# Three edits where a graph-attention kernel passes from projections to gathers

## Chip, cores and metric

The kernel runs on one core of one Trainium2 chip. The time is the device time of one execution in microseconds; three runs of the kernel before gave 1809.18, 1814.11 and 1813.44 us, median 1813.44 us. The engines are TensorE (PE in the profile, its weight loads PEld), VectorE (DVE), ScalarE (ACT), GpSimd (POOL) and SyncE (SP). Each works through its own queue in order; an instruction that waits holds up all behind it. SyncE, ScalarE and GpSimd also issue transfers.

## The reference

One layer of attention over a graph of 4096 nodes with 512 features and 8 heads of 64, float32 throughout:

```python
hs, ht = layer_norm(x), layer_norm(h_target)
q = (ht @ Wq + bq) / sqrt(64); k = hs @ Wk + bk; v = hs @ Wv + bv
logits = where(adj != 0, q . k, -1e30)            # per head, 4096 x 4096
ht = ht + (softmax(logits) @ v) @ Wo + bo
ht = layer_norm(ht)
out = layernorm(x + ht + gelu(ht @ W1) @ W2)      # W1: 512 x 2048
```

adj is sparse: a row has about 17 entries, at most some 39.

## The kernel before

The kernel does not form the 4096 x 4096 logits. It has two phases.

**Phase 1.** The function `project` goes through x in 16 groups of two tiles of 128 rows. For each tile, `source` multiplies the normed, transposed rows by Wk and Wv (L929), ScalarE copies the two halves out of PSUM (L931), and ScalarE's queue writes the k|v rows, 128 x 1024, to the table `kvd` in DRAM (L935). At the same time `edges` turns adj into lists of neighbours, tile by tile of 128 rows, each in four quarters of 1024 columns: SyncE loads a quarter (`quarter`, L713), ScalarE takes its sign and counts it (L728), VectorE multiplies by positions (L733) and takes the eight largest of five segments (L735); at a tile's end VectorE merges them (L742 to L759), and the leftover goes to DRAM (L766). There are 32 tiles, so 128 quarters; I number the quarters 0 to 127. After the first 16 tiles (half A), `sort` ranks the rows by degree, and GpSimd scatters the lists as records to DRAM (L853, 16 transfers). After these, `first_fronts` starts the q rows of the first two sorted tiles.

**Phase 2.** `attention` takes the sorted tiles in 211 chunks of up to three neighbours. GpSimd gathers the k|v rows of each neighbour, 128 rows of 4 KB, from `kvd` into slots of a ring (L966); VectorE multiplies k by q (L1220) and sums by head (L1225); ScalarE takes exp and scales a third of the values (L1204); VectorE scales the others (L1184); TensorE sums the values by transposing products into PSUM (L1192). `finish` and `feed` do Wo, the second norm and the feed-forward part (L1325, L1334). The lists of half B that are not yet made are made meanwhile.

**The ring.** `ring` has 20 slots of 1024 floats for each partition. In phase 1 it is lent out: slots 0 to 7 hold adjacency quarters (`DEEP` = 8), 8 to 11 rows of h_target and later 8 to 10 the last k|v rows, 12 to 16 rows of x (`xrows`). Slots 17 and 18 are `wide`; quarters from tile NA + FILL on take these two in turn, so the load of a quarter waits until the sign of the quarter two before it has been taken. In phase 2 the gathers of half A use slots 0 to 16, and `place` says which slots each chunk gets; a chunk that doesn't fit before the end of the ring starts again at 0.

**Order.** The generators are woven together by the costs that they yield; a scheduler then sets the order in each engine's queue. Two things steer it near the change. `fill` makes `FILL` tiles of half B's lists in phase 1; `other_lists` makes the rest. And `front`, which makes the q rows of a tile, begins with a tie: VectorE's L994 reads the norm factors in the record and, formally, the tile named in `latest`, so it can't come before that tile is there. ScalarE's L998 then scales the gathered row, TensorE transposes it (L1002), ScalarE copies (L1005), TensorE multiplies by Wq (L1011), VectorE adds the bias (L1016). `latest` is set in `source`, and `first_fronts` goes on as soon as it is set:

```python
tie = nc.vector.scalar_tensor_tensor(m, m, latest[-1], m, op0=ALU.bypass, op1=ALU.max)
...
while not latest:
    yield None
```

Of the kernel before, what the change touches and what calls it, by code (L numbers as in the profile page):

```python
# [423 lines left out]
def _take(gen, n):  # L424

    for _ in range(n):
        cost = next(gen, StopIteration)
        if cost is StopIteration:
            return
        yield cost  # L430
# [13 lines left out]
def adj_resnorm_kernel(  # L444
# [38 lines left out]
    NT = N // P  # L483
    G = 2
# [48 lines left out]
    with tc.tile_pool(name="keep", bufs=1) as keep:  # L533
# [17 lines left out]
        with ExitStack() as late:  # L551
# [151 lines left out]

            adjs = []
            DEEP = 8
            FILL = 5

            def quarter(i, h):
                if i < NA + FILL:
                    a = ring[:, (i * NQ + h) % DEEP, :].bitcast(I32)  # L710
                else:
                    a = turn_of("wide", wide)
                nc.sync.dma_start(a, adj[i * P:(i + 1) * P, h * QW:(h + 1) * QW])  # L713
                return a

            def edges(i):
# [4 lines left out]
                for h in range(NQ):  # L721
# [7 lines left out]
                    ahead = min(n + DEEP - 1, n + 3 + n // 2)  # L729
                    while len(adjs) < min(max(n + 3, min(ahead, (NA + FILL) * NQ)), NT * NQ):  # L730
                        adjs.append(quarter(*divmod(len(adjs), NQ)))
# [132 lines left out]
            def project(order, t=None):  # L864
# [54 lines left out]
                def source(n, j):  # L919
                    g, hT = order[n], state[n][1]  # L920
                    if asked or moms:
                        kvr = sp.tile([P, 2 * D], F32, name="tq", bufs=3)
                    else:

                        kvr = ring[:, 8 + (n * G + j) % 3, :]
                    for half, w in enumerate((wk, wv)):
                        pkv = psi.tile([P, D], F32, name="pq", bufs=3)
                        for kc in range(KC):
                            nc.tensor.matmul(pkv, hT[:, kc, j * P:(j + 1) * P], w[:, kc, :],  # L929
                                             start=kc == 0, stop=kc == KC - 1)  # L930
                        nc.scalar.copy(kvr[:, half * D:(half + 1) * D], pkv)  # L931
                    if n >= 14:
                        latest[:] = [kvr[:, 0:1]]
                    r0 = 1 + (g * G + j) * P
                    newest[:] = [nc.scalar.dma_start(kvd[r0:r0 + P, :], kvr).ins]  # L935
                    return 7.8
# [13 lines left out]
                for n in range(len(order)):  # L950
                    for j in range(G):
                        cost = source(n, j)
                        if j == 0:
                            request(n + 4)
                            measure(n + 3)
                            turn(n + 1)
                        else:
                            scale(n + 2)
                            del state[n]
                        yield cost  # L960
# [9 lines left out]
            def prefetch(i):  # L970
                if i >= NT or i in recs:
                    return
                r0 = TILES[i][0]
                part = 1 if r0 >= PARTS[1][0] * P else 0
                assert part in done
                r0 -= PARTS[part][0] * P
                rec = sp.tile([P, E0 + MAXE], I32, name="rec", bufs=6)

                nc.gpsimd.dma_start(rec[:, :RW], recs_d[part][r0:r0 + P, :])
                recs[i] = rec  # L980

            def front(i, idle=0):


                rec = recs[i]
                tq = sp.tile([P, 2 * D], F32, name="tq", bufs=3)
                t = tq[:, :D]
                gather(t, h_target, rec[:, TGT:TGT + 1])
                for _ in range(1 + idle):
                    yield  # L990


                m = rec[:, RST:RST + 2].bitcast(F32)
                tie = nc.vector.scalar_tensor_tensor(m, m, latest[-1], m, op0=ALU.bypass,  # L994
                                                     op1=ALU.max)
                with tc.issue_after(tie.ins):
                    nc.vector.tensor_copy(tags[:, i, :], rec[:, DEG:TGT + 1])
                nc.scalar.activation(t, t, AF.Identity, bias=m[:, 1:2], scale=m[:, 0:1])  # L998
                yield
                pt = ps.tile([P, KC, P], F32, name="t", bufs=2)  # L1000
                for kc in range(KC):
                    nc.tensor.transpose(pt[:, kc, :], t[:, kc * P:(kc + 1) * P], ident)  # L1002
                hT = tq[:, D:].rearrange("p (c t) -> p c t", c=KC)
                for kc in range(KC):
                    nc.scalar.activation(hT[:, kc, :], pt[:, kc, :], AF.Identity,  # L1005
                                         bias=b1r[:, kc:kc + 1], scale=s1c[:, kc:kc + 1])
                yield
                yield
                pq = ps.tile([P, D], F32, name="t", bufs=2)
                for kc in range(KC):  # L1010
                    nc.tensor.matmul(pq, hT[:, kc, :], wq[:, kc, :], start=kc == 0,  # L1011
                                     stop=kc == KC - 1)
                yield
                yield
                yield
                nc.vector.scalar_tensor_tensor(tq[:, :D], pq, HD ** -0.5, bqr,  # L1016
                                               op0=ALU.mult, op1=ALU.add)
                tqs[i] = tq

            EARLY = 2  # L1020
# [1 line left out]
            SG = [(i, j0, min(S, cap - j0)) for i, (_, cap) in enumerate(TILES)  # L1022
                  for j0 in range(0, cap, S)]
            kvs, rests, fronts = {}, {}, {}
            place = [0]
            for i, _, n in SG:
                if place[-1] + n > RING[i >= NA]:
                    place[-1] = 0
# [6 lines left out]
            def step(gens, i):  # L1035

                if i in gens and next(gens[i], StopIteration) is StopIteration:
                    del gens[i]
# [111 lines left out]
            def go_on():  # L1150
                for i in list(fronts):
                    step(fronts, i)

            def first_fronts():

                for i in range(EARLY):
                    prefetch(i)
                for i in range(EARLY):
                    fronts[i] = front(i)
                    step(fronts, i)  # L1160
                while not latest:
                    yield None
                while fronts:
                    go_on()
                    yield 4.0
# [235 lines left out]
            def prepare():  # L1401

                yield from _take(ed, NA * steps)
                ready.append("lists")
                while moms:
                    moments(moms.pop(0))
                rs, nm = rstd_of(wp, mvh, NT, "n0")
                for R, (i0, n) in zip(Rs, PARTS):
                    Rf = R.bitcast(F32)
                    nc.vector.tensor_copy(Rf[:, :, RST], rs[:, i0:i0 + n])  # L1410
                    nc.vector.tensor_copy(Rf[:, :, RST + 1], nm[:, i0:i0 + n])
                nm = turn_of("wide", wide)
                nc.sync.dma_start(nm[:NT, :P], nodemask.rearrange("(c p) -> c p", p=P))
                nmf = nm.bitcast(F32)[:NT, P:2 * P]
                nc.vector.tensor_scalar(nmf, nm[:NT, :P], 1.0, None, op0=ALU.not_equal)
                nc.vector.tensor_reduce(bad[:NT, 0:1], nmf, AX.X, ALU.max)
                yield from sort(0)
                yield from first_fronts()

            def fill():  # L1420
# [3 lines left out]
                yield 9.0  # L1424
                for cost in _take(ed, FILL * steps):
                    yield cost
# [60 lines left out]
```

## Time and profile before

| | before |
|---|---|
| median of three runs | 1813.44 us |
| the profiled execution, its span | 1811.19 us, 1809.4 us |
| TensorE busy, of the span | 1681.5 us, 93% |
| VectorE, ScalarE, GpSimd busy | 1435.1, 1221.1, 979.8 us |
| moved from and to DRAM | 463.26 MB, mean 256 GB/s |
| last k\|v row's write issued (L935) | 290.03 us |
| first gather of k\|v rows issued (L966) | 296.81 us |
| first attention multiply (L1220) | 308.02 us |

Times in the timeline are microseconds from the start of the span. A line of it gives the start, the duration, the engine, the line of the program and the operation; in brackets at the end stand how long the engine had been idle, and what ended that. Lines with a letter q (SPq, ACTq) are transfers being issued. A wait for several things is put down to the one that the profile saw end last. The table of windows gives busy microseconds for each engine in a stretch of time, with the number of instructions, the granted clock of TensorE (1.00 is full) and the share of the DMA engines that was busy.

### The profile page before, as it was taken

The page shows a single profiled execution, that of the slowest core. Times are in us where ns is not written, and L with a number is a line of the kernel's source. Part 1 is how long each engine was busy: PE and PEld are TensorE (multiplying, and loading weights), DVE is VectorE, ACT ScalarE, POOL GpSimd, SP SyncE. Part 2 cuts the span into 40 slices and gives each one's busy share as a digit, 9 for nine tenths or more (in the row PEclk, how much of TensorE's full clock was granted, in tenths as well). Part 3 has the DMA queues.
Part 4 walks back from the last instruction along what each step waited for, and adds up shares of the span by engine and source line. Part 5 has one row for each costly group of instructions (what it writes and reads, how often), then busy time and mean ns, then how long its engine had stood idle before and what let it go on. Part 6 is the DMA issues. An engine that isn't in the chain of part 4 may idle for free. (4 is left out here: it accounts for less than half of the span.)

```text
span 1809.4 us, 22969 instructions
## 1 busy us (share of the span) xinstructions
PE 1681.5 (93%) x7030; PEld 1101.4 (61%) x7030; DVE 1435.1 (79%) x2660; ACT 1221.1 (67%) x3119; POOL 979.8 (54%) x834
## 2 busy tenths in 40 slices
PE   7989984587999989999999989999999999999997
PEld 3434432465766666676776757666666666666664
DVE  6989886899999837777879989979879797988200
ACT  5767654486997636767768867877777676787211
POOL 1000144666566576667767788877575665663101
PEclk9999996698999999999999999999999999999998
DMA  9999968988887647778879888787776777774000
GB/s 343 370 376 375 344 228 293 405 276 321 294 300 237 230 159 258 240 253 279 281 256 320 288 263 292 252 281 261 242 273 216 255 239 247 247 246 149 18 6 26
DMA packets 140268, 463.26 MB, mean 256 GB/s; under 512 B 16500, under 2 KB 21672, under 8 KB 140136
## 3 DMA queue, kind: packets, MB, share of 16 engines
q0 software_dynamic: 96656, 342.64, 55.9%
q1 hardware_dynamic: 35664, 95.98, 15.0%
q10 hardware_dynamic: 7816, 23.08, 3.3%
q8 instruction: 58, 0.95, 0.2%
q14 instruction: 74, 0.61, 0.1%
HBM read 430.75 MB, written 30.89 MB: 255 GB/s over the span
## 5 line engine op out<-in xcount | busy, mean ns | idle before, releaser
L966 POOL DMA_INDIRECT kv<-kvd,rec x603 | 761.1, 1262 | 366.9 <-PE cps L1192 147.8
L1334 PE MATMUL po<-w,gt 128*128 128x512 f32 x1024 | 466.9, 598 | 10.3 <-ACT gt L1328 10.3
L1325 PE MATMUL pf<-h2T,w 128*128 128x256 f32 (+1 forms) x2176 | 466.5, 368 | 0.0
L1325 PEld LDWEIGHTS pf<-h2T,w 128*128 128x128 f32 x2176 | 389.7, 191 | 64.4 <-issue 19.8
L1220 DVE TENSOR_TENSOR kv<-kv,tq 128x1536 f32<-128x1536 f32 (+2 forms) x211 | 352.0, 1677 | 62.0 <-DMA kv<-kvd,rec 57.9
L1204 ACT ACTIVATE kv<-kv,pa 128x64 f32<-128x64 f32 x1520 | 390.9, 337 | 4.5
L1225 DVE TENSOR_REDUCE lg<-kv 128x24 f32<-128x1536 f32 (+2 forms) x211 | 350.4, 1668 | 1.2
L1334 PEld LDWEIGHTS po<-w,gt 128*128 128x128 f32 x1024 | 189.1, 192 | 207.2 <-issue 195.3
L1192 PE MATMUL cps<-ident,kv 128*128 128x128 f32 x2008 | 267.8, 282 | 47.7 <-DVE kv L1184 40.0
L1192 PEld LDWEIGHTS cps<-ident,kv 128*128 128x128 f32 x2008 | 242.2, 146 | 114.0 <-DVE kv L1184 45.8
L1184 DVE TENSOR_TENSOR kv<-kv,p 128x1024 f32<-128x1024 f32 (+1 forms) x211 | 251.3, 1195 | 23.8 <-ACT p L1229 22.5
L687 POOL TENSOR_TENSOR n_rs<-n_ve,mhalf 128x2 f32<-128x2 f32 (+2 forms) x51 | 48.6, 953 | 326.0 <-DVE n_ve L680 173.0
L728 ACT ACTIVATE kv<-kv 128x1024 uint8<-128x1024 int32 x128 | 134.9, 1055 | 94.5 <-DMA kv<-in_adj_dram 42.9
L1328 ACT ACTIVATE gt<-pf 128x512 f32<-128x512 f32 x128 | 76.3, 597 | 87.4 <-PE pf L1325 84.0
L1328 ACT ACT_TABLE_LOAD x103 | 132.1, 1283 | 1.7
L735 DVE MAX8 cand<-kv 128x8 uint16<-128x103 uint16 (+1 forms) x640 | 132.4, 253 | 0.5
L929 PE MATMUL pq<-wk,h2T 128*128 128x512 f32 x256 | 121.3, 619 | 8.3 <-ACT tq L931 5.7
L1229 ACT ACTIVATE p<-lg 128x24 f32<-128x24 f32 (+2 forms) x179 | 39.1, 218 | 120.5 <-DVE lg L1225 119.7
L1011 PE MATMUL t<-wq,tq 128*128 128x512 f32 x256 | 115.7, 595 | 2.1 <-ACT tq L1005 2.1
L929 PE MATMUL pq<-wv,h2T 128*128 128x512 f32 x256 | 115.4, 593 | 1.8 <-DVE rbc L662 1.0
L1115 PE MATMUL t<-wo,rb 128*128 128x512 f32 x256 | 115.2, 592 | 0.0
L929 PEld LDWEIGHTS pq<-wk,h2T 128*128 128x128 f32 x256 | 49.4, 199 | 65.3 <-issue 50.5
(160 smaller groups left out, 1581.8 us busy)
## 6 DMA issues: line engine op xcount, KB each, us to landing
kv<-in_adj_dram SPq DMA_DIRECT2D x128, 512.0 KB, 7.1
kvd<-tq ACTq DMA_DIRECT2D x24, 512.0 KB, 6.6
kv<-kvd,rec POOLq DMA_INDIRECT x603, 5.9
kv<-in_L_gnn_h_target_dram SPq DMA_DIRECT2D x32, 256.0 KB, 8.0
kv<-in_x_dram SPq DMA_DIRECT2D x15, 512.0 KB, 9.3
rest_d<-gid SPq DMA_DIRECT2D x32, 160.0 KB, 4.7
w<-in_L_gnn_W_dram SPq DMA_DIRECT2D x4, 1024.0 KB, 9.9
kvd<-kv ACTq DMA_DIRECT2D x8, 512.0 KB, 5.2
```

The lines of the kernel that those rows point to most:

```text
L728: nc.scalar.activation(sg, a, AF.Sign, accum_out=dpart[:, i, h:h + 1])
L735: nc.vector.max(cand[:, h * SQ + s, :], wd[:, w0:w1])
L929: nc.tensor.matmul(pkv, hT[:, kc, j * P:(j + 1) * P], w[:, kc, :], start=kc == 0, stop=kc == KC - 1)
L966: nc.gpsimd.indirect_dma_start(out=dst, out_offset=None, in_=table[:, :], in_offset=bass.IndirectOffsetOnAxis(ap=idx, axis=0))
L1184: nc.vector.tensor_tensor(v4, v4, p[:, j0:j0 + m, :].unsqueeze(3) .to_broadcast([P, m, H, HD]), ALU.mult)
L1192: nc.tensor.matmul(cps[:, c, :], kv[:, j, D + c * P:D + (c + 1) * P], ident, is_transpose=True, start=j0 + j == 0 and c == 0, stop=j0 + n ...
L1204: newest[:] = [nc.scalar.mul(v, v, pa[:, hd:hd + 1]).ins]
L1220: nc.vector.tensor_tensor(kv[:, :n, :D], kv[:, :n, :D], tq[:, :D].unsqueeze(1).to_broadcast([P, n, D]), ALU.mult)
L1225: nc.vector.tensor_reduce(lg[:, :n, :], kv[:, :n, :D].rearrange("p j (h d) -> p j h d", h=H), AX.X, ALU.add)
L1325: nc.tensor.matmul(pf[:, k, :], w1[(f0 + k) // KC][:, kc, (f0 + k) % KC * P:((f0 + k) % KC + 1) * P], h2T[:, kc, :w], start=kc == 0, stop= ...
L1328: nc.scalar.activation(gt, pf, AF.Gelu_apprx_tanh)
L1334: nc.tensor.matmul(po[j], gt[:, k, j * P:(j + 1) * P], w2[(f0 + k) // KC][:, (f0 + k) % KC, :], start=False, stop=f0 + k == FC - 1, skip_g ...
```

## The change

There are four edits. `FILL` goes from 5 to 4, so tile 20 of the lists is left to `other_lists` and its quarters use the two wide slots. `latest` is set only by the very last k|v row, where it was set by each row of the last two groups. The first chunk's gathers start at ring slot 11 in place of 0, so the first two chunks take slots 11 to 16, and all later places shift. And the loops that fetch the first two records and start the first two fronts are merged.

```diff
             DEEP = 8
-            FILL = 5
+            FILL = 4
...
-                    if n >= 14:
+                    if n * G + j == NT - 1:
                         latest[:] = [kvr[:, 0:1]]
...
-            place = [0]
+            place = [11]
             for i, _, n in SG:
                 if place[-1] + n > RING[i >= NA]:
                     place[-1] = 0
...
                 for i in range(EARLY):
                     prefetch(i)
-                for i in range(EARLY):
                     fronts[i] = front(i)
                     step(fronts, i)
                 while not latest:
```

## The prediction, before the result was known

> **What bounds the kernel now.** I read the windows first: busy time of each engine by stretch, with the granted clock and the DMA share.
>
> ```profile
> core 0: us, PE busy (x) PEld busy (x) DVE busy (x) ACT busy (x) POOL busy (x), PEclk, DMA share, GB/s
> 297.00:350.00 53.00, 15.90 (x64) 12.87 (x65) 40.08 (x68) 20.99 (x71) 35.61 (x30) 0.50 1.02 392
> 400.00:450.00 50.00, 40.83 (x205) 29.43 (x204) 48.95 (x112) 33.95 (x96) 32.67 (x27) 0.86 0.88 314
> 450.00:500.00 50.00, 50.00 (x227) 35.20 (x226) 46.13 (x109) 45.63 (x110) 27.64 (x23) 1.00 0.85 288
> 1500.00:1600.00 100.00, 100.00 (x434) 68.32 (x434) 81.25 (x94) 72.59 (x192) 62.66 (x53) 1.00 0.76 256
> ```
>
> Three regimes follow one another. From the first gather (297) to 350 the transfers are the bound: DMA share 1.02, TensorE busy 15.9 of 53 us at half clock. To about 450 VectorE is (48.95 of 50), fed by attention and by the lists still to be made. After that TensorE is full to the end: 1403 of the 1459 us from 350 on are busy. So a microsecond by which the first gather moves should reach the end nearly whole. What sets the first gather is in the timeline, ahead of it:
>
> ```profile
> 262.61 1.06 ACT L728 ACTIVATE kv<-kv 128x1024 uint8<-128x1024 int32 x1 [2.23 <-DMA kv<-in_adj_dram]
> 268.84 0.22 DVE L994 SCALAR_TENSOR_TENSOR rec<-rec,kv 128x2 f32<-128x2 f32 x1 [6.78 <-DMA rec<-rec]
> 273.06 0.81 ACT L998 ACTIVATE tq<-tq,rec 128x512 f32<-128x512 f32 x1 [9.30 <-DVE gid L750]
> 273.93 1.11 PE L1002 MATMUL t<-ident,tq 128*128 128x128 f32 x4 [7.91 <-ACT tq L998]
> ...
> 286.82 0.62 ACT L931 COPY kv<-pq 128x512 f32<-128x512 f32 x1
> ...
> 290.03 0.33 ACTq L935 DMA_DIRECT2D kvd<-kv  x1
> ...
> 296.81 0.96 POOL L966 DMA_INDIRECT kv<-kvd,rec  x1 [20.42 <-ACT kv L728]
> ...
> 308.02 1.77 DVE L1220 TENSOR_TENSOR kv<-kv,tq 128x1536 f32<-128x1536 f32 x1 [1.98 <-DMA kv<-kvd,rec]
> ```
>
> The tie (L994) stands in VectorE's queue long before its record has landed: VectorE stops 6.78 us, ScalarE 9.30, TensorE 7.91, and the last two k|v rows stand behind them. The last row is copied from 286.82, its write to kvd issued at 290.03, landed 6.0 us later by the answer for that line, and 0.8 us after that POOL issues the first gather. The page names ScalarE's L728 as releaser; but the adjacency quarters that held slots 0 to 2 were read by 248.7, so I take the landing, which all gathers need.
>
> **What the skill says.** The Trainium skill, "DMA: Bandwidth & Descriptors", section "Issuing engines are not separate DMA queues": transfers of ScalarE, SyncE and GpSimd run on the same 16 engines and interleave. The trace agrees: share 1.02 while all three issue. "Anatomy of one DMA — SWDGE (gpsimd) path" gives about 2.0 us plus bytes/436e3. For a 512 KB quarter that is, as an estimate, 3.2 us, below the 3.8 to 6.3 us measured here; I use the measured ones. "TensorE: Matmul & The Clock Gate", section "What's actually happening": half clock after an idle window of some 3.4 us. The trace agrees (PEclk 0.50 from 297 to 350), and it costs nothing there, since DMA is the bound.
>
> **The change, part by part**, against the profiled execution's 1811.19 us (span 1809.4; the median shown is 1813.44, 2.25 above it; gains are taken from the median).
>
> *The tie.* The compiled order puts L994 and L998 behind the copy of the last row's k half (L931), and TensorE's L1002 behind both products of that row. L994 now waits for a record that landed at 268.8 at the latest, so the 6.78, 9.30 and 7.91 us go. Behind the tie stand the maxima of later lists, which nobody needs there; behind L998 stands the row's v half, which then waits for the quarter ahead of it, below.
>
> *FILL 5 to 4.* Quarters 80 to 83 (tile 20) leave the eight slots and take the two wide ones, which before began at 84. A wide quarter costs a round trip: sign 1.06, 0.12 until SyncE issues the load of the next but one (254.54 to 254.66), landing, 0.1. Four landings of quiet time can be read: 3.8 (issued 242.3), 6.3 (256.2), 5.5 (276.85 to the sign at 282.38), 4.6 (279.4): mean 5.0, so 6.3 us for each two quarters. ScalarE's queue after the change holds quarters 80 to 92 among the last copies; SyncE's loads follow in their order. From 80 at 245.6 and 81 at 246.7: 82 at 251.9, 83 at 253.6 (behind a copy), 84 at 258.2; then two copies and four L914 (3.2 us), 85 at 262.7; 86 at 264.5, 87 at 269.0, 88 at 270.8, 89 at 275.3, 90 at 277.1. The last row's k half is copied at 278.2; 91 at 281.6, two L998 to 284.2, 92 at 284.2, v half copied at 285.3, its write issued at 286.0. Before: 290.03. Gain 4.0; the first gather at about 292.8. TensorE follows: three pq buffers let the last row's products run at 269 to 276, before the copies want them. The eight L1005 and L1011 end at about 294, ahead of the first gathered rows (292.8 plus 11.2, as 296.81 to 308.02 before).
>
> *Work handed on.* VectorE's order has 97 quarters ahead of the sixth gathered chunk in both versions; after it, the changed kernel is 3 quarters behind at the 24th chunk (105 against 108) and level at the 30th (116). A quarter costs VectorE 0.41 + 0.93 us and a quarter of a tile's 4.1 us end: 2.4. So VectorE has up to 7.2 us less to do where it is the bound (TensorE waits some 9 us between 428 and 442) and 7.2 more from 460 to 520, where it had about 4 us free. The bounds are 7 gained and 3 lost; I take 1 gained, since most returns soon.
>
> *place = [11].* Six first chunks still have 17 slots of their own; slots 11 to 16 were last read by transposes or as h rows that are long done. The adjacency waits of the first gathers go, but they were not the last to end: 0. If they had been, 1 to 2 us. Counting over all 211 chunks, a slot's last user lies five chunks back for 54 of A's chunks (56 before), and never nearer: 0.
>
> *The merged loop.* The compiled POOL queue still has five record loads and then the three row gathers: 0. The x gathers for the end (2 x 1 us on POOL) now wait for the later tags, at about 280, and stand ahead of the first gather; they end by 283, before 292.8. A landing that came 10 us sooner would uncover them.
>
> Sum: 4.0 + 1 = 5 us, 1806.2 for the profiled execution, **1808.4 against the median**.
>
> **Rivals.** *The two slots take the tie's place*: each microsecond of landing is paid about five times in the chain 80, 82, ... 92. At 5.8 us the gain is nil: 1813.4. For it: 6.3 is in the trace, when a row's write was in flight; against: 3.8 and 4.6 as well. *Slower*: the same chain, place ScalarE's queue from 246 to 290, at the 7.1 us measured with the DMA full (222 to 226): 11 us later instead of 4 earlier, so 7 lost, 1820. It decides from a mean landing of 6.8 us on (5.4 lost). Against it: these 13 quarters and some rows are about 10 MB in 45 us, some 220 GB/s, where the windows from 45 to 180 moved 370. *VectorE's relief stays*: the early chunks gain most of the 7.2 us and the later ones pay it from slack: 4 + 7, so 1802. For it: TensorE's 9 us of waits; against: VectorE at 46 to 49 of 50 us right after. *The change does nothing*, because L728 is the true releaser: then removing it gains too, so that isn't apart from the first case.
>
> **How the numbers follow.** Likeliest 0.50, 1808.4, with its own range 1804 to 1812; no gain 0.20; slower 0.15; relief 0.15. About 0.3%, 5.4 us, is what a measurement of this kernel can tell from no change: faster lies below 1808.0. Faster: 0.50 x 0.5 + 0.15 = 0.40. Slower, above 1818.9: 0.15, and 0.03 of the others for an order on TensorE that I can't cost. Same 0.42. The range reaches from the relief to the slow chain: 1799 to 1820.
>
> **What would show it.** Right: no 7 us gap at L994, L998 or L1002; the last kvd write at about 286; the first gather at about 293 with the landing or nothing behind it; L728 waiting for adjacency loads about ten times for 3 to 5 us between 246 and 290; the first L1220 at 304; from there the same windows some 4 us sooner. Wrong: ScalarE's waits of 5 us and more for quarters 82 to 92, or an L998 that waits for its tie to be freed; or TensorE idle for more than 16 us between 400 and 500, from list work that now falls there.

## The result, and the profile after

| | before | after |
|---|---|---|
| median | 1813.78 us (4 runs, 1809.18 to 1814.74) | 1831.51 us (4 runs, 1826.58 to 1834.99) |
| the profiled execution, its span | 1811.19 us, 1809.4 us | 1834.99 us, 1833.2 us |
| last k\|v row's write issued (L935) | 290.03 us | 287.02 us |
| first gather of k\|v rows issued (L966) | 296.81 us | 293.90 us |
| first attention multiply | 308.02 us | 304.48 us |

The changed kernel is slower: after over before is 1.0101, 95% interval 1.0071 to 1.0131. Forecast were 1808.4 us, with a range from 1799 to 1820. From line 1158 on the changed program's numbers are one lower: L1220 of before is L1219 of after, L1225 is L1224, L1334 is L1333.

The start came out within 1.1 us of the forecast at all three of these times. These are lines of the timeline of after:

```profile
251.03 1.06 ACT L728 ACTIVATE kv<-kv 128x1024 uint8<-128x1024 int32 x1 [3.89 <-DMA kv<-in_adj_dram]
...
258.13 1.06 ACT L728 ACTIVATE kv<-kv 128x1024 uint8<-128x1024 int32 x1 [3.77 <-DMA kv<-in_adj_dram]
...
283.28 1.50 ACT L998 ACTIVATE tq<-tq,rec 128x512 f32<-128x512 f32 x2
...
284.13 1.97 PE L1002 MATMUL t<-ident,tq 128*128 128x128 f32 x8 [8.08 <-ACT tq L998]
...
287.02 0.33 ACTq L935 DMA_DIRECT2D kvd<-kv  x1
...
293.90 0.94 POOL L966 DMA_INDIRECT kv<-kvd,rec  x1 [11.50 <-DMA rest_d<-gid]
...
304.48 1.76 DVE L1219 TENSOR_TENSOR kv<-kv,tq 128x1536 f32<-128x1536 f32 x1 [7.03 <-DMA kv<-kvd,rec]
```

The stalls of 6.78 and 9.30 us at L994 and L998 are gone; ScalarE waits instead for the loads through two slots, 3.9 and 3.8 us here, and all the same issues the last row 3.0 us sooner. TensorE still waits ahead of L1002, 8.08 us (7.91 in before), but the products of all k|v rows now stand ahead of that wait. So the loss lies later. The windows of after show where:

```profile
core 0: us, PE busy (x) PEld busy (x) DVE busy (x) ACT busy (x) POOL busy (x), PEclk, DMA share, GB/s
400.00:450.00 50.00, 37.86 (x188) 27.87 (x187) 46.28 (x96) 35.34 (x105) 34.25 (x28) 0.83 0.90 322
450.00:500.00 50.00, 48.88 (x221) 34.48 (x220) 43.12 (x102) 41.37 (x98) 26.18 (x21) 1.00 0.76 257
500.00:550.00 50.00, 44.64 (x187) 29.46 (x188) 46.40 (x115) 40.34 (x99) 24.02 (x20) 0.93 0.72 245
600.00:700.00 100.00, 92.11 (x420) 63.74 (x419) 75.42 (x91) 59.33 (x166) 56.36 (x49) 0.97 0.61 201
```

and of before, for the two stretches that the prediction did not show:

```profile
500.00:550.00 50.00, 48.15 (x213) 32.39 (x212) 49.43 (x123) 43.18 (x105) 29.53 (x24) 1.00 0.88 306
600.00:700.00 100.00, 92.97 (x414) 63.20 (x413) 62.34 (x72) 59.16 (x164) 67.01 (x61) 0.97 0.59 199
```

From 400 to 450 VectorE was relieved (46.28 us busy instead of 48.95), and TensorE did less, not more (37.86 instead of 40.83). From 500 to 550 TensorE is busy 3.5 us less. From 600 to 650 it is 4.8 us less (43.89 against 48.69), but from 600 to 700 only 0.9. What it waits for after 600 is in the timeline of after:

```profile
598.11 0.92 DVE L735 MAX8 cand<-kv 128x8 uint16<-128x103 uint16 x5
...
604.46 0.96 DVE L827 TENSOR_TENSOR kv<-kv,bins 128x768 bf16<-128x768 bf16 x1
605.33 0.68 DVE L1016 SCALAR_TENSOR_TENSOR tq<-t,bqr 128x512 f32<-128x512 f32 x1
...
618.28 0.81 ACT L1133 ACTIVATE h<-h,n_nm,n_rs 128x512 f32<-128x512 f32 x1 [1.16 <-DVE n_nm L692]
...
623.10 1.04 PE L1142 MATMUL t<-ident,h 128*128 128x128 f32 x8
...
630.04 1.93 ACT L1146 ACTIVATE h2T<-t,cols 128x256 f32<-128x256 f32 x4
...
631.11 1.12 PE L1098 MATMUL t<-ident,rb 128*128 128x128 f32 x4 [6.11 <-ACT h2T L1146]
632.02 5.28 PE L1333 MATMUL po<-w,gt 128*128 128x512 f32 x6
```

and the same chain in before:

```profile
586.88 0.95 DVE L827 TENSOR_TENSOR kv<-kv,bins 128x768 bf16<-128x768 bf16 x1
...
591.67 0.69 DVE L1016 SCALAR_TENSOR_TENSOR tq<-t,bqr 128x512 f32<-128x512 f32 x1 [3.09 <-PE t L1011]
...
604.63 0.81 ACT L1133 ACTIVATE h<-h,n_nm,n_rs 128x512 f32<-128x512 f32 x1 [0.83 <-DVE n_nm L692]
...
614.25 1.04 PE L1142 MATMUL t<-ident,h 128*128 128x128 f32 x8
...
616.39 1.93 ACT L1146 ACTIVATE h2T<-t,cols 128x256 f32<-128x256 f32 x4
...
617.46 0.66 PE L1098 MATMUL t<-ident,rb 128*128 128x128 f32 x4 [1.31 <-ACT h2T L1146]
```

After is 13.7 us late at L1016 and 13.65 at ScalarE's h of the second norm (L1133) and at its h2T (L1146), the transposed rows for the feed-forward part. TensorE's transposes of h (L1142) are only 8.85 us late and done at 624.1; h2T comes at 630.04, because it stands in ScalarE's queue behind the exps and scales of two chunks, and ScalarE has no gap between L1133 and L1146. In before, VectorE had the lists behind it by then, and at L1016 it waited 3.09 us for TensorE. In after, the last quarter's maxima (L735, at 598), its tile's end and the first step of the second sort (to L827) stand in VectorE's queue ahead of L1016, and nothing is left of that margin. TensorE was 8.85 us late at L1142; the other 4.8 are the wait of 6.11 in place of 1.31.

This wait is no net loss, though. Before has one like it 36 us later, for ScalarE's gelu (gt), which after has not; hence the 0.9 us from 600 to 700:

```profile
667.49 5.29 PE L1334 MATMUL po<-w,gt 128*128 128x512 f32 x6 [5.43 <-ACT gt L1328]
```

What stays lost lies one group earlier, where the same links show in after,

```profile
503.98 1.76 DVE L735 MAX8 cand<-kv 128x8 uint16<-128x103 uint16 x10
...
508.54 0.68 DVE L1016 SCALAR_TENSOR_TENSOR tq<-t,bqr 128x512 f32<-128x512 f32 x1
...
525.10 0.16 DVE L692 SCALAR_TENSOR_TENSOR n_nm<-mv,n_rs 128x2 f32<-128x2 f32 x1 [0.62 <-POOL n_rs L687]
...
533.25 1.11 PE L1098 MATMUL t<-ident,rb 128*128 128x128 f32 x4 [4.54 <-ACT h2T L1146]
```

and in before:

```profile
502.44 0.68 DVE L1016 SCALAR_TENSOR_TENSOR tq<-t,bqr 128x512 f32<-128x512 f32 x1
...
514.00 0.16 DVE L692 SCALAR_TENSOR_TENSOR n_nm<-mv,n_rs 128x2 f32<-128x2 f32 x1 [0.57 <-POOL n_rs L687]
...
527.53 0.66 PE L1098 MATMUL t<-ident,rb 128*128 128x128 f32 x4 [1.85 <-ACT h2T L1146]
```

The maxima of two quarters stand in one row at 503.98, L1016 is 6.1 us late, the norm's last step on VectorE (L692) 11.1, and TensorE's wait is 4.54 us in place of 1.85.

VectorE's compiled order shows how the lists came there. In before, one quarter (its L733) stands between the 30th and 31st chunk, three between the 36th and 37th, none between the 42nd and 43rd. In after these are five, seven and three. The 30th, 36th and 42nd chunk end a tile. The multiplies of the traces say the same: after is 1.1 us ahead at the 30th (494.46 against 495.55), 10.55 us behind at the 37th (560.06 against 549.51), 13.65 at the 43rd (606.05 against 592.40).

### The profile page after: what moved, and what is told of

Same layout as the page of the kernel before. It is cut to its first block, busy times and chain, and to the rows that moved or that the text cites. A ratio compares the mean times of both kernels' runs of the same rounds, so it can differ in the third digit from the quotient of the medians.

```text
span 1833.2 us, 22964 instructions
## 1 busy us (share of the span) xinstructions
PE 1691.0 (92%) x7030; PEld 1103.2 (60%) x7030; DVE 1437.3 (78%) x2660; ACT 1217.3 (66%) x3115; POOL 985.4 (54%) x834
## 5 line engine op out<-in xcount | busy, mean ns | idle before, releaser
L966 POOL DMA_INDIRECT kv<-kvd,rec x603 | 763.0, 1265 | 354.9 <-PE cps L1191 142.9
L1333 PE MATMUL po<-w,gt 128*128 128x512 f32 x1024 | 469.5, 601 | 7.3 <-ACT gt L1327 7.3
L1219 DVE TENSOR_TENSOR kv<-kv,tq 128x1536 f32<-128x1536 f32 (+2 forms) x211 | 351.9, 1677 | 83.3 <-DMA kv<-kvd,rec 71.6
L1224 DVE TENSOR_REDUCE lg<-kv 128x24 f32<-128x1536 f32 (+2 forms) x211 | 350.1, 1668 | 1.3
L1333 PEld LDWEIGHTS po<-w,gt 128*128 128x128 f32 x1024 | 190.2, 193 | 205.8 <-issue 196.6
L687 POOL TENSOR_TENSOR n_rs<-n_ve,mhalf 128x2 f32<-128x2 f32 (+2 forms) x51 | 52.5, 1029 | 338.3 <-DVE n_ve L680 183.0
L735 DVE MAX8 cand<-kv 128x8 uint16<-128x103 uint16 (+1 forms) x640 | 132.1, 253 | 0.7
L1011 PE MATMUL t<-wq,tq 128*128 128x512 f32 x256 | 119.4, 610 | 8.7 <-ACT tq L1005 8.7
```

Source lines behind the costliest of these rows:

```text
L735: nc.vector.max(cand[:, h * SQ + s, :], wd[:, w0:w1])
L966: nc.gpsimd.indirect_dma_start(out=dst, out_offset=None, in_=table[:, :], in_offset=bass.IndirectOffsetOnAxis(ap=idx, axis=0))
L1219: nc.vector.tensor_tensor(kv[:, :n, :D], kv[:, :n, :D], tq[:, :D].unsqueeze(1).to_broadcast([P, n, D]), ALU.mult)
L1224: nc.vector.tensor_reduce(lg[:, :n, :], kv[:, :n, :D].rearrange("p j (h d) -> p j h d", h=H), AX.X, ALU.add)
L1333: nc.tensor.matmul(po[j], gt[:, k, j * P:(j + 1) * P], w2[(f0 + k) // KC][:, (f0 + k) % KC, :], start=False, stop=f0 + k == FC - 1, skip_g ...
```

## The experiments

Single executions of one kernel lie 5 us and more from their median, and two traces of the changed kernel have spans of 1833.2 and 1824.4 us. So differences are taken between medians or ratios, and traces only for the place of a loss. Ratios are to the kernel before on the same chip. "The tie" below is the change to `latest`.

**The edits one by one, and FILL undone.** Theory A: the lists handed on by FILL cost. B: the gather slots (place). C: no edit carries it, only compiled orders.

```diff
-            FILL = 5
+            FILL = 4
```


> The kernel before with FILL 4 alone (tie and place as before). Theory A, list work: the quarters that the two slots make three later return after the first group of tiles, when TensorE is already the bound, so this edit alone carries the loss: 1826 to 1836 us, with TensorE's busy time per 50 us down by 3 to 5 us somewhere between 430 and 700. Theory B, ring: the offset of the gather slots carries it, so this is 1811 to 1817. Theory C, order: no edit carries it alone, the compiled orders of VectorE and ScalarE differ with each, and this is anywhere in 1808 to 1826.

```diff
-                    if n >= 14:
+                    if n * G + j == NT - 1:
```


> The kernel before with the tie moved to the last k|v row alone. Every theory: the 7 us gaps of VectorE, ScalarE and TensorE at L994, L998 and L1002 go, and the last write to kvd is issued 3 to 8 us sooner than 290.0, since no two-slot chain stands in its way. A and B: this reaches the end, 1805 to 1811. C: it may reach the end or be lost, 1805 to 1822.

```diff
-            place = [0]
+            place = [11]
```


> The kernel before with the first gathers' slots begun at 11 alone. Theory A: 1811 to 1817, nothing. Theory B: slots whose readers are still at work hold gathers back, 1826 to 1836, with VectorE's wait for gathered rows 10 us and more above the 57.9 of the kernel before. Theory C: 1808 to 1826, with no gather that waits for its slot.

The last starts from the changed kernel:

```diff
-            FILL = 4
+            FILL = 5
```


> The changed kernel with FILL set back to 5 (tie, place and the merged loop stay). Theory A: the loss goes and the gain of the start stays, 1804 to 1811. Theory B: the loss stays, 1826 to 1836. Theory C: somewhere between, 1808 to 1830, and not the sum of the single edits.

| run | median us | ratio, 95% interval |
|---|---|---|
| FILL alone | 1825.51 | 1.0067 (1.0042 to 1.0091) |
| tie alone | 1807.29 | 0.9964 (0.9950 to 0.9978) |
| place alone | 1817.35 | 1.0024 (1.0012 to 1.0035) |
| all but FILL | 1811.72 | 0.9984 (0.9967 to 1.0002) |

FILL carries most of the loss and the tie is a gain, as A says, though FILL alone stayed 0.5 us short of its band and the run without FILL lies 0.7 above its own. The tie's write to kvd was issued at 287.28, 2.75 us sooner than before, where 3 to 8 were expected, and TensorE's wait ahead of L1002, which was expected to go, is 9.51 us. FILL alone starts late: its first multiply comes at 312.37, 4.35 us after that of before, and its TensorE is busy 8.7 us less from 600 to 650, where A had 3 to 5. Place costs about 4, which A had as nothing, and far less than B had. Without FILL, tie and place add up: -6.2 and +3.9 make -2.3, measured -1.8.

**What of FILL costs.** FILL 4 does two things: four quarters more go through the two wide slots, and the stream of later lists is one tile longer, so everything in it, the second sort too, comes 18 units later (four quarters at 3, a tile's end at 6) in the plan that weaves it with attention, where a group of two tiles counts 60. The first run has the tie and FILL together (and the merged loop); the other three start from the tie alone and separate the two.

```diff
-            place = [11]
+            place = [0]
```


> The changed kernel with place set back to 0: the tie and FILL 4 together. If the three edits' effects add (tie 6.2 gained, FILL 12.0 lost, place 3.9 lost, from the single edits) this is 1819, and the changed kernel should have been 1823. If the two slots take the tie's gain in the start, so that FILL costs more beside the tie, this is 1825 to 1829, and place is the rest.

```diff
-                if i < NA + FILL:
+                if i < NA + FILL - 1:
...
-                    while len(adjs) < min(max(n + 3, min(ahead, (NA + FILL) * NQ)), NT * NQ):
+                    while len(adjs) < min(max(n + 3, min(ahead, (NA + FILL - 1) * NQ)), NT * NQ):
```


> The kernel with the tie on the last row alone (1807.3), where tile 20's quarters also take the two wide slots, as with FILL 4, but all lists keep their planned times, as with FILL 5. Theory of the two slots: what FILL costs is the chain of loads through two slots ahead of the first gather, so this is 1816 to 1823, with the last write to kvd 4 us or more later than without. Theory of the delay: the cost is that lists, the second sort and its scatters are planned 18 units later, so this is 1804 to 1812.

```diff
-            WAIT = 40.0
+            WAIT = 58.0
```


> The kernel with the tie on the last row alone (1807.3), with FILL 5 and every slot as it was, but with the other lists' stream begun at 58 units in place of 40: the 18 units (4 quarters of 3 and a tile's end of 6) by which one tile more delays it. Theory of the delay: 1816 to 1823, with the second sort at the 51st chunk, its last scatter at 700 us or later in place of 661, and TensorE waiting for h2T or rb of a tile's end between 500 and 660. Theory of the two slots: 1804 to 1811.

```diff
-            FILL = 5
+            FILL = 4
...
-            WAIT = 40.0
+            WAIT = 22.0
```


> The kernel with the tie on the last row alone (1807.3), with FILL 4, and the other lists' stream begun at 22 units in place of 40, so that each later list and the second sort keep the places that they have with FILL 5. Theory of the delay: the loss goes, 1804 to 1812. Theory of the two slots: the loss stays, 1816 to 1823.

| run | median us | ratio, 95% interval |
|---|---|---|
| tie and FILL 4 | 1821.80 | 1.0046 (1.0029 to 1.0063) |
| tie, wide slots from tile 20 on | 1810.13 | 0.9983 (0.9970 to 0.9997) |
| tie, lists 18 units later | 1820.65 | 1.0045 (1.0029 to 1.0061) |
| tie, FILL 4, lists 18 units sooner | 1812.09 | 0.9987 (0.9971 to 1.0003) |

This decides it. With five tiles made ahead, the same slots and the same work, the delay alone costs 13.4 us; FILL 4 without the delay costs 4.8, of which the slots are 2.8 (the intervals touch that of the tie alone). The two slots are out as the main cause. The parts overlap: 4.8 and 13.4 make 18.2, where FILL 4 whole costs 14.5 beside the tie. The tie and FILL together lie between the sum of the single edits (1819) and the case that the slots take the tie's gain (from 1825), nearer to the sum. The windows of the tie alone,

```profile
420.00:450.00 30.00, 20.49 (x91) 15.52 (x89) 30.00 (x58) 19.60 (x57) 19.83 (x17) 0.77 0.94 347
500.00:550.00 50.00, 48.21 (x217) 32.67 (x216) 49.44 (x115) 42.15 (x100) 27.49 (x22) 1.00 0.86 305
```

and of the tie with the delay:

```profile
420.00:450.00 30.00, 17.48 (x96) 13.24 (x95) 25.46 (x41) 20.19 (x57) 20.74 (x16) 0.83 0.95 355
500.00:550.00 50.00, 44.16 (x187) 29.43 (x186) 43.99 (x103) 39.68 (x96) 18.72 (x18) 0.93 0.69 239
```

From 420 to 450 VectorE is freed of 4.5 us, and TensorE loses 3.0; from 500 to 550 TensorE loses 4.1, though VectorE is busy 5.5 us less. In after the same freedom was not used either: its TensorE waited 6.80 us for rb, a tile's inverse softmax sums, at 432 (2.68 in before) with the DMA share at 0.96 from 420 to 450 (0.93 in before).

How far TensorE is behind the tie alone, at the first matrix product of each tile's end (L1111), in single traces, in us, tiles counted from 0:

| tile in order | 2 | 4 | 5 | 7 | 8 | 11 | 31 |
|---|---|---|---|---|---|---|---|
| tie with the delay | 1.4 | 1.7 | 9.4 | 18.1 | 10.5 | 14.6 | 13.7 |
| the changed kernel | 0.1 | 4.1 | 10.3 | 20.8 | 13.2 | 20.1 | 22.5 |

The delay alone draws the curve of the changed kernel: up at tile 5, up at tile 7, that second rise back at tile 8, and up at tile 11. The rise at 5 is the link shown at 533; that at 7 is the wait at 631 (630.3 with the delay), and it goes back because the tie alone has its own wait later, 4.82 us for ScalarE's gelu at 664.64. The cause of the rise at 11 stays open. The last scatter of the tie with the delay came at 717.7 us, where the tie alone has 660.5.

**The changed kernel again, the sort alone late, and lists sooner.** The first run is unaltered; the others start from the tie alone.

> The changed kernel once more, unaltered, so that its time stands beside the others' with as many runs. The tie and FILL 4 together gave 1821.8. If place costs beside them what it costs alone (3.9) or beside the tie (4.4), this is 1824 to 1828; if it costs the whole distance to the first measurement, 1830 to 1834.

```diff
                 keep_rest()
+                yield 18.0
                 yield from sort(1)
```


> The kernel with the tie alone (1807.3) with 18 units of pause put ahead of the second sort: the lists keep their places, the sort goes from the 48th chunk to the 51st as with the delay of everything (1820.7). If the loss comes from the lists' own maxima, which stand in VectorE's queue ahead of a group's end, this is 1806 to 1811. If it comes from the sort, its 16 scatters and the records they write, 1815 to 1822.

```diff
-            WAIT = 40.0
+            WAIT = 22.0
```


> The kernel with the tie alone (1807.3), FILL 5, with the other lists' stream begun at 22 units in place of 40: the opposite of the delay, lists and sort some 3 to 6 chunks sooner. If a later stream simply costs and an earlier one gains, this is 1797 to 1804. If 40 is near the best, because before 450 VectorE has no room, it is 1807 to 1818, with VectorE full and TensorE idle between 400 and 450.

```diff
-            FILL = 5
+            FILL = 6
```


> The kernel with the tie alone (1807.3) with FILL 6: one tile of lists more made ahead, and all later ones 18 units sooner. Theory of the delay, as for the stream begun at 22 units: the compiled order of VectorE puts the same quarters at the same chunks, so this is within 3 us of that run; theory of the amount made ahead: it is 5 us or more better than that run.

| run | median us | ratio, 95% interval |
|---|---|---|
| the changed kernel again | 1828.98 | 1.0089 (1.0062 to 1.0116) |
| tie, sort alone later | 1805.27 | 0.9940 (0.9920 to 0.9961) |
| tie, lists 18 units sooner | 1808.81 | 0.9968 (0.9953 to 0.9983) |
| tie, FILL 6 | 1812.85 | 0.9985 (0.9964 to 1.0005) |

A later sort costs nothing (it came out 0.7 below its band): it is the lists. Their loads, signs and maxima move together in all these runs; that the maxima do it is read from the traces and shown by no run. The changed kernel itself lies between its two bands. Sooner lists gain nothing. FILL 6 missed its band of 3 us above or below the run with sooner lists by 1 (4.0 higher), with overlapping intervals; that more lists made ahead would help is out. The tie with the later sort beats both kernels; against the tie alone its intervals overlap.

**Late, or stacked? And place.** Two more starts for the stream, from the tie alone, and two more places, in the changed kernel.

```diff
-            WAIT = 40.0
+            WAIT = 64.0
```


> The kernel with the tie alone (1807.3), FILL 5, the other lists' stream begun at 64 units. It is later than at 58 (1820.7; the sort at the 52nd chunk instead of the 51st), but its compiled order spreads the lists: quarters 112 to 115 stand between the 30th and 35th chunk, and 120 to 123 between the 36th and 40th, where at 58 eight quarters stand at the 30th and eight at the 36th. Theory of lateness: 1820 to 1826. Theory of stacking: 1809 to 1816.

```diff
-            WAIT = 40.0
+            WAIT = 46.0
```


> The kernel with the tie alone (1807.3), FILL 5, the other lists' stream begun at 46 units: a third of the delay of 58, with the sort at the 48th chunk as without. Its order has four quarters at the 30th chunk and eight between the 35th and 36th. Theory of lateness: about a third of the loss, 1809 to 1814. Theory of stacking: between, 1810 to 1817, with the loss at the 36th chunk and none at the 30th.

```diff
-            place = [11]
+            place = [14]
```


> The changed kernel with place 14 instead of 11: the first chunk still goes to slots that held x, and the slots of all later chunks are shifted as well. Its compiled order has quarters 112 to 115 at the 35th chunk, as with place 0 (1821.8), where place 11 has them at the 30th (1829 to 1831). Theory that place acts through the lists' position: 1818 to 1825. Theory that it acts through the slots: 1827 to 1833.

```diff
-            place = [11]
+            place = [3]
```


> The changed kernel with place 3 instead of 11: no slot of x is used for the first chunk, but the slots are shifted against place 0. The lists stand as with place 0. Theory of the lists' position: 1818 to 1825. Theory that any shift of the slots costs: 1826 to 1833.

| run | median us | ratio, 95% interval |
|---|---|---|
| tie, stream from 64 | 1823.53 | 1.0046 (1.0029 to 1.0063) |
| tie, stream from 46 | 1818.28 | 1.0033 (1.0022 to 1.0044) |
| changed kernel, place 14 | 1829.32 | 1.0100 (1.0070 to 1.0131) |
| changed kernel, place 3 | 1828.21 | 1.0082 (1.0055 to 1.0108) |

Stacking is not decided. The run at 64 was to spread the lists, but in its trace five quarters stand between the 30th and 31st chunk and six between the 36th and 37th, as many as at 58. FILL alone speaks against it, with two and three there and 12.0 us lost, of which 4.35 ahead of its first multiply. Lateness is right in kind, not in proportion: a third of the delay (46) has most of the loss, more than either theory gave it. TensorE's one wait, summed from 480 to 660, grows with these four starts (the trace at 46 is of an execution of 1814.41 us, 3.9 below its median). The columns are the total, the number of waits, the longest; the traces are those of the stream begun at 40,

```profile
PE t L1098 <- ACT h2T L1146: 3.1, 2, 1.8
```

at 46,

```profile
PE t L1098 <- ACT h2T L1146: 5.8, 2, 4.4
```

at 58,

```profile
PE t L1098 <- ACT h2T L1146: 9.2, 2, 6.1
```

and at 64:

```profile
PE t L1098 <- ACT h2T L1146: 11.6, 2, 7.5
```

It does not measure the loss, though. With the stream begun at 22 it is 7.9, and that run is within 2 us of the one begun at 40:

```profile
PE t L1098 <- ACT h2T L1146: 7.9, 2, 6.3
```

So how the late lists come to cost TensorE 13 us is shown only in part, at 533.

For place, the lists' position is out: with 3 and 14 the lists stand nearly as with place 0, yet it is 1828 to 1829 and not 1821.8. So are the slots of x for the first gathers: place 3 gives the first three chunks none of them and costs the same. What remains is that each shift of the slots that was tried costs: the three values other than 0 cost 6 to 10 us beside the tie and FILL 4. How it does that stays open: no single place in the traces shows it.

**Undoing one thing in the changed kernel itself.**

```diff
-            WAIT = 40.0
+            WAIT = 22.0
```


> The changed kernel with all its edits, but with the other lists' stream begun at 22 units in place of 40, which gives the later lists and the second sort the places that they had before. If the delay is the main cause of its loss, this is 13 us or more below the changed kernel (1829 to 1831): 1811 to 1818. If place or the two slots carry it, 1822 to 1831.

```diff
-                    if n * G + j == NT - 1:
+                    if n >= 14:
```


> The changed kernel with the tie put back on the last two groups of rows, FILL 4 and place 11 kept. If the tie gains in it what it gains alone (6.2) or beside FILL 4 (3.7): 1832 to 1837. If its gain at the start is swallowed by the late lists: 1827 to 1832.

| run | median us | ratio, 95% interval |
|---|---|---|
| changed kernel, lists 18 units sooner | 1816.69 | 1.0039 (1.0023 to 1.0055) |
| changed kernel, old tie | 1842.46 | 1.0167 (1.0143 to 1.0191) |

With the lists back in time, 12.3 us (against the second measurement of the changed kernel) to 14.8 (against the first) return; by ratios, each to the kernel before on its own chip, 9 to 11. The wait is back to where it was:

```profile
PE t L1098 <- ACT h2T L1146: 2.5, 2, 1.3
```

The old tie costs 11 to 13.5 in the changed kernel, about twice what it costs alone (6.2): beyond its band. Its first multiply comes at 310.16, 5.7 us after that of the changed kernel. So the tie's gain is not swallowed, and the sizes depend on each other.

## Why the prediction was wrong, step by step

- **What bounds the kernel, and the first gather.** Held in kind: with the tie alone the gain of the start reaches the end. It is not one for one: the first multiply came at 305.19, 2.8 us sooner, and the median is 6.2 lower.
- **The tie.** Held but for TensorE's 7.91 us, which did not go (8.08 at L1002) and cost nothing that I can see: no stall at L994 or L998, last write 287.02 (forecast 286.0), first gather 293.90 (292.8), first multiply 304.48 (304).
- **FILL, the chain through two slots.** Held in the start: quarters 82, 85, 88 and 91 were taken at 251.03, 261.98, 270.68 and 282.23, forecast 251.9, 262.7, 270.8 and 281.6. The slower rival put the loss here; the loss came, but from here only 2.8 us, with the tie.
- **Work handed on: the step that failed.** I had bounds of 7 gained and 3 lost and took 1 gained, "since most returns soon". The delay alone measured 13.4 lost. Three things were wrong. I counted quarters per chunk up to the 30th, where after was "level" only with the five quarters that stand behind that chunk (ahead of it, as I had counted at the 24th, it is 112 against 116), and did not go on: the 36th and 42nd chunk take seven and three. I priced the work by room, "about 4 us free" against 7.2, where position counts: behind the lists in VectorE's queue stands the chain of a group's second norm, which in before has no margin at 502 and 3.09 us at 592. The traces show that at 533; for the rest of the 13.4 us the way to TensorE stays open. And I booked a relief ahead of 450 as TensorE's gain; VectorE idled instead. The case for the relief as a rival falls with it.
- **place = [11].** Taken as 0, which failed too; it is 3.9 alone and 7 to 10 in the changed kernel, from a cause that stays open. That a slot's last user is never nearer was no reason for zero.
- **The merged loop.** Taken as 0 and never run alone. It is in the run without FILL, whose time is the sum of the other two edits within 0.5 us, so nothing speaks for a cost.
- **The sum.** With measured terms: tie -6.2, FILL without the delay +4.8, delay +13.4, place +3.9, together +15.9; measured +15.2 to +17.7 (1828.98 and 1831.51 against 1813.78). Since the terms depend on each other (FILL's two make 18.2 apart and 14.5 together), the fit is no proof. My 0.03 for an order that I could not cost was far too little, and a sign that I named, 16 us of TensorE idle between 400 and 500, looked too early: it was idle 13.3 there (9.2 before), and the larger part came after 500.

## What to carry to other kernels

Work moved behind a phase boundary is priced not only by the free time of the engine that takes it, but also by what stands behind it in that engine's queue: follow the chain from there to the bounding engine, and find its margin. A longer wait in the trace of after is a loss only if before has not its like a little later. When a stream is planned by a running cost, one item more at its head delays every later item, so count to the stream's end. When an edit moves a buffer index through a whole loop, give it a range, even where no wait can be named.

## What the runs showed of the hardware that I had not expected

A wait of TensorE cost more than its length here. After the 6.11 us in after, four L1098 took 1.12 us (0.66 in before) and six L1333 5.28 us, where eight at 614 took 3.60. The window just after it, in after:

```profile
631.00:636.00 5.00, 4.89 (x9) 2.60 (x10) 2.27 (x3) 4.64 (x14) 0.00 (x0) 0.50 0.52 195
```

The granted clock is 0.50. Six at 0.45 would be 2.7, so the clock adds 2.6 + 0.5 = 3.1 us to this wait. Before pays the same after its 5.43 us at 667 (six in 5.29 us), so between the two kernels it cancels. The Trainium skill, "TensorE: Matmul & The Clock Gate", section "What's actually happening", says that an idle window of about 3.4 us brings half clock. The traces agree in part: the waits of 1.31 and 1.85 us in before were followed by full speed, but in the tie with the delay one of 2.41 us, with 0.38 more right behind it, was followed by a clock of 0.50 (527 to 529). In the prediction I used that section for the start, where it costs nothing, and not for new waits in the stretch where TensorE is the bound.
